# Down projection of an fp4-gated attention kernel: three of five full chunks per token tile as three one-pass products

## The chip, the cores and the metric

The kernel runs on one NeuronCore of a Trainium2 chip. The core has a matrix engine (PE, with its weight loads shown apart as PEld), a vector engine (DVE), a scalar engine (ACT), a general engine (POOL) and a queue engine (SP) that here issues nearly all DMA transfers. Each engine runs its own list of instructions in the order of the program and waits on semaphores for the others. The metric is the device time of one execution in microseconds (us). The kernel before was measured three times: 646.16, 646.59 and 648.52 us, median 646.59 us. A difference of some 0.5% (about 3 us) is what such a measurement can tell from none.

## What is computed

The input `x` has 4 batches of 2048 tokens with 256 values each. Layer normalisation gives `xn`. A linear attention with norms over the tokens gives `s`. A gated feed-forward net, all of whose operands are rounded block by block (16 values) to fp4, gives `g`; the result is `x + s * silu(g)`.

```python
def fp4_linear(x, w):
    xq = fp4_quant_dequant(x)
    wq = fp4_quant_dequant(w)
    return jnp.einsum('bsk,nk->bsn', xq, wq)
gate = fp4_linear(x, w_gate)
y = fp4_linear(x, w_up)
h = jax.nn.silu(gate) * y          # 704 values of a token
return fp4_linear(h, w_down)       # 704 -> 256
...
xn = _layernorm(x, axis=-1)
s = _L0_attn_ref(xn, ...)
g = _silu(_L0_ffn_ref(xn, ...))
x = x + s * g
```

A rounded value is a block's scale (its largest magnitude over 6) times one of fifteen grid values. The last line of the feed-forward net, the product with `w_down`, is the down projection that the change is about.

## The kernel before

**Tiling.** Tokens go in 32 groups of 256 (`N` = 32), each as two token tiles of 128 (`T` = 2); eight groups make a batch. One step `s` of the main loop (line 1084) works on several groups at once: gate and up products of group `s+1`, scaling and rounding of `h` of group `s-1`, the down projection of group `s-3`, layer normalisation and the Gram matrix of group `s+3`, the attention's product for group `s-7`. Loops are written out in full, and each engine's order is the order of the text, by hand.

**Gate and up.** A group has six pieces (3 chunks of weights by 2 token tiles), u0 to u5. From group 6 on all of them run as products of exact parts: `x = a + b` with `a` its upper part (a product with `1 - 2**-13`, stored in the one-pass format fp32r), `m = a - 4096 b`, and likewise for the weights. `gu_begin` (line 532) issues four one-pass products (a with the first part, b with the second, for two halves of the 256 values), then ACT scales the PSUM bank in place by `1 + 1/4096` (line 550); `gu_end` (line 553) adds two products with `m` and ACT takes silu (line 570). Then `h` is the product of the two halves, on DVE (`times_up`, line 581) for the first pieces and on POOL (line 577) for the last two.

**h.** `scale_h` (line 445) takes the largest magnitude of each block (line 165, DVE), the inverse scales (lines 174 and 178), and writes the scaled `h` into a tile `y` of its own (line 188), and with it the scaled `xn` of a later group. ACT shortens the upper halves of these words to 16 bits (`short_part`, line 227, three instructions), DVE rounds them to the grid (line 237). The scales themselves are transposed (`turn_scales`, line 464), written to DRAM, and read back by two broadcasts into the tile `se` (`spread_scales`, line 475): first the part for `xn` (256 KB), then that for `h` (704 KB). A step later `rescale_h` (line 521) transposes the eleven chunks of 128 values (two token tiles of five full chunks each, and one chunk shared by both) and multiplies them by `se` into `hqt` (line 527). `rescale_x` (line 496) does the same for `xn`, and `part_a`, `part_b`, `part_m` (lines 505 to 519) split it into the parts that the gate and up products take.

**Down projection.** `down` (line 609) takes for each token tile five plain fp32 products of 128 by 128 by 256, each of which the profile records as two instructions (line 617), and two one-pass products for the shared middle chunk (line 627), whose halves `part_middle` (line 593) has made with ACT and POOL. In the steady loop the parts of `down` stand at three places of the step: after the Gram matrix, before u2, and after u1's end. `gate_of` (line 636) takes silu out of PSUM. Five groups later `close` multiplies by the attention's result (line 676, DVE), POOL adds `x` (line 683), and SP stores.

**What sets the order around the change.** In one step DVE goes: the last part of `part_m`, the two reductions of `scale_h`, line 174, line 178, line 188 twice, `times_up` of u0, `close`, `times_up` of u1, `rescale_x`, `on_grid`, `times_up` of u2 and u3, `rescale_h`, `part_b`, `part_m`. ACT goes: the bank scaling of u0, `part_middle`, the bank scaling of u1, two sums of a later group, silu of u0, the transposed scales, `short_part` three times, the bank scaling of u2, silu of u1, and so on. Three steps out of eight carry a batch's attention algebra as well (`attention`, line 703, advanced by calls of `turn()`): its products, and on DVE its elementwise work, stand between `part_m` of one step and `scale_h` of the next.

**Buffers.** A tile name with `bufs` buffers is handed out again when all readers of the older tile are through; who writes the new tile waits for them. Before, `se`, `f`, and each of `xq0`, `xq1`, `xq2` (the parts a, b, m of `xn`) have two buffers, `hqt` one, `h` three.

## Time and profile before

| | |
|---|---|
| times | 646.16, 646.59, 648.52 us; median 646.59 us |
| span of the profiled execution | 647.0 us |
| busy: PE, DVE, ACT, POOL | 613.8, 477.7, 420.4, 183.7 us |
| mean granted clock of PE | 0.995 |
| a step without attention work | 17.0 us (start of line 638 at 343.99, 361.02, 378.08, 395.10 us) |
| the three steps with it | 21.23, 20.74, 20.97 us (line 638 at 412.23, 433.46, 454.20, 475.17 us) |
| products of line 617 / line 627 | 640 records / 128 records |

The page gives no time of its own for the profiled execution apart from the span, which lies 0.4 us above the median of the times. Times in the trace are from the start of the span. A record's duration reaches from its start to its modelled end; records of PE overlap, so the distance between starts, not the duration, says what a product costs in a stream.

### The profile page before, as it was taken

How to read it: one execution, taken by the hardware profiler on the slowest of the kernel's cores; microseconds unless marked ns; L12 is line 12 of the kernel's file. 1: busy time of each engine (PE TensorE's matmuls, PEld its weight loads, DVE VectorE, ACT ScalarE, POOL GpSimd, SP SyncE). 2: the span in 40 equal slices, each digit the busy share in tenths (PEclk: the TensorE clock that was granted, in tenths of full speed). 3: DMA queues.
4: the chain of work that ended last, by engine and by line, in shares of the span. 5: the costliest groups of instructions: out<-in, count | busy, mean ns of one | idle time of the engine just before them, and what ended most of it. 6: DMA issues, size and time to landing. Idle time of an engine off the chain costs nothing. (4 is left out here: it accounts for less than half of the span.)

```text
span 647.0 us, 9702 instructions
## 1 busy us (share of the span) xinstructions
PE 613.8 (95%) x3267; PEld 501.7 (78%) x3269; DVE 477.7 (74%) x942; ACT 420.4 (65%) x1108; POOL 183.7 (28%) x291
## 2 busy tenths in 40 slices
PE   4799898999899999999999999999999999999997
PEld 2446566778788888878788888878788888888886
DVE  6767767596777778596787868597786868686663
ACT  3457778666677777667677777756677766655431
POOL 4566684212122212112122222113122122113113
PEclk9899899999999999999999999999999999999999
DMA  9210043332233444442344444423443333322233
GB/s 208 89 34 16 19 102 94 79 81 60 57 88 111 115 111 112 115 90 70 73 112 113 114 115 113 109 60 75 101 115 98 97 94 103 92 67 67 83 94 131
DMA packets 29287, 59.47 MB, mean 92 GB/s; under 512 B 3541, under 2 KB 9909, under 8 KB 29237
## 3 DMA queue, kind: packets, MB, share of 16 engines
q1 hardware_dynamic: 28964, 58.59, 35.5%
q8 instruction: 26, 0.43, 0.3%
q10 hardware_dynamic: 272, 0.26, 0.1%
q14 instruction: 25, 0.20, 0.1%
HBM read 48.57 MB, written 10.27 MB: 91 GB/s over the span
## 5 line engine op out<-in xcount | busy, mean ns | idle before, releaser
L550 ACT ACTIVATE gu<-gu 128x512 f32<-128x512 f32 (+1 forms) x160 | 89.0, 556 | 139.8 <-PE gu L546 139.3
L546 PE MATMUL gu<-wgu,xq 128*128 128x512 f32 (+1 forms) x640 | 176.1, 397 | 2.8 <-DVE h L581 2.1
L617 PE MATMUL dn<-wdt,hqt 128*128 128x256 f32 x640 | 154.8, 382 | 0.5 <-ACT gate L1258 0.5
L577 POOL TENSOR_TENSOR h<-si,up 128x192 f32<-128x192 f32 (+1 forms) x92 | 67.0, 731 | 269.2 <-ACT up L576 269.1
L546 PEld LDWEIGHTS gu<-wgu,xq 128*128 128x128 f32 x640 | 113.2, 188 | 19.7 <-DVE h L581 3.2
L617 PEld LDWEIGHTS dn<-wdt,hqt 128*128 128x128 f32 x640 | 115.4, 190 | 16.5 <-ACT gate L1258 0.7
L581 DVE TENSOR_TENSOR h<-si,gu 128x256 f32<-128x256 f32 x100 | 41.8, 418 | 87.9 <-ACT si L570 87.9
L560 PE MATMUL gu<-wgu,xq 128*128 128x512 f32 (+1 forms) x320 | 99.5, 392 | 0.5 <-ACT gu L550 0.5
L570 ACT ACTIVATE si<-gu 128x256 f32<-128x256 f32 (+1 forms) x192 | 69.6, 363 | 19.6 <-PE gu L546 17.2
L683 POOL TENSOR_TENSOR gate<-gate,xl 128x512 f32<-128x512 f32 x27 | 34.5, 1278 | 120.6 <-issue 96.9
L560 PEld LDWEIGHTS gu<-wgu,xq 128*128 128x128 f32 x320 | 59.3, 188 | 10.5 <-ACT gu L550 1.6
L227 ACT ACTIVATE t_h<-y_h 128x704 f16<-128x704 bf16 (+2 forms) x86 | 60.7, 770 | 7.8 <-DVE y_h L188 7.7
L666 PE MATMUL at<-M,xnt 128*128 128x256 f32 x256 | 65.3, 384 | 0.0
L527 DVE TENSOR_TENSOR hqt<-tp_qh,se 128x1024 f32<-128x1024 f16 x64 | 53.8, 883 | 14.7 <-PE tp_qh L493 11.5
L398 PEld LDWEIGHTS gram<-xn 128*128 128x128 f32 x256 | 44.2, 194 | 15.9 <-ACT xn L373 8.2
L398 PE MATMUL gram<-xn 128*128 128x257 f32 (+1 forms) x256 | 48.7, 334 | 7.5 <-ACT xn L373 7.5
L546 PE MATMUL gu<-wp,xqt 128*128 128x512 f32 (+1 forms) x120 | 52.2, 581 | 2.2 <-ACT xqt L385 2.2
L188 DVE SCALAR_TENSOR_TENSOR y_h<-h,inv_h 128x1408 f32<-128x1408 f32 x32 | 53.5, 1671 | 1.1
L165 DVE TENSOR_REDUCE scs<-h 128x88 f32<-128x1408 f32 x32 | 51.5, 1610 | 0.0
L666 PEld LDWEIGHTS at<-M,xnt 128*128 128x128 f32 x256 | 45.9, 190 | 4.0
L601 POOL TENSOR_TENSOR both<-hqt,both 64x128 fp32r<-64x128 f32 x56 | 31.8, 568 | 42.8 <-ACT both L599 40.6
L546 PEld LDWEIGHTS gu<-wp,xqt 128*128 128x128 f32 x120 | 22.7, 199 | 23.1 <-issue 16.1
(176 smaller groups left out, 916.5 us busy)
## 6 DMA issues: line engine op xcount, KB each, us to landing
se<-there SPq DMA_DIRECT2D x32, 704.0 KB
x<-in_L_attn_x_dram SPq DMA_DIRECT2D x32, 256.0 KB
out_dram<-gate SPq DMA_DIRECT2D x31, 256.0 KB
se<-there SPq DMA_DIRECT2D x27, 256.0 KB
xl<-in_L_attn_x_dram SPq DMA_DIRECT2D x27, 256.0 KB
there<-sct SPq DMA_DIRECT2D x27, 60.0 KB
wd_n<-in_L_ffn_w_down_dram SPq DMA_DIRECT2D x1, 704.0 KB
wgu_n<-in_L_ffn_w_up_dram SPq DMA_DIRECT2D x2, 256.0 KB
```

What stands on the lines that cost most here:

```text
L165: nc.vector.tensor_reduce(sc, src.rearrange("p a (n k) -> p a n k", k=BLK), AX.X, ALU.max, apply_absolute_value=True)
L188: nc.vector.scalar_tensor_tensor(y.rearrange("p (a n k) -> p a n k", a=a, k=BLK), src.rearrange("p a (n k) -> p a n k", k=BLK), DOWN, inv. ...
L227: nc.scalar.activation(t[:, lo:hi], upper[:, lo:hi], AF.Copy, scale=ONE * (1.0 + 2.0**-8))
L398: nc.tensor.matmul(grams[b][:, o : o + L + 1 - c * P], xn[:, t, c * P : (c + 1) * P], xn[:, t, c * P : L + 1], start=(g == 0 and t == 0 an ...
L527: nc.vector.tensor_tensor(ht[:, cols], turn_chunks(q, g0, g1, f"h{n}"), spread_sc[n][:, cols], ALU.mult)
L546: nc.tensor.matmul(gu[:, : nb * P], x_k, w_k, start=(k == 0), stop=(k == len(pairs) - 1), skip_group_check=True)
L550: nc.scalar.activation(gu[:, : nb * P], gu[:, : nb * P], AF.Copy, scale=1.0 + 1.0 / STEP)
L560: nc.tensor.matmul(gu[:, : nb * P], xqt[n][2][:, t, c, :], wgu[2][:, c, cols], start=False, stop=(c == KC - 1), skip_group_check=True,)
L570: nc.scalar.activation(si[:, :nb, :], pair[:, :, 0, :], AF.Silu)
L577: nc.gpsimd.tensor_tensor(h, si[:, :nb, :], up[:, :nb, :], ALU.mult)
L617: nc.tensor.matmul(ods[n][:, t, :], hqt[n][:, t * (half + 1) + i, :], wdt[:, t * half + i, :], start=(i == 0), stop=False, skip_group_chec ...
L666: nc.tensor.matmul(ready[n][:, t, :], xnt[n][:, c, t * P : (t + 1) * P], M[:, c, :], start=False, stop=(c == KC - 1), skip_group_check=True,)
```

## The change

Of the five full chunks of each token tile three (`KX` = 3, so six of ten per group) are no longer plain fp32 products. Their `h` is split into exact parts as the gate and up products do it: `split_a` (ACT, 128x768), `split_b` (POOL, `h - a`) and `split_m` (DVE, `a - 4096 b`), and the weights into three parts (`split_d`, once, in the opening stage). The down projection of a group becomes `down_first` (six one-pass products per token tile), `down_scale` (ACT scales the PSUM bank in place by `1 + 1/4096`), and `down_rest` (two one-pass products for the middle chunk, two plain fp32 ones, three one-pass ones with `m`, per token tile). The first piece u1 is issued ahead of the first part of the down projection. Scaled `h` is written in place over `h`, so the tile `y` goes; scaled `xn` goes to a smaller tile. Buffers become single for `se`, `xq1`, `xq2`, and `f`, and the reading back of the scales moves behind `rescale_h`, the last reader of the older `se`. `rescale_h` writes two tiles with three instructions, chunks to be split first. At the end the two token tiles of the last group get a PSUM bank each.

```diff
@@ scale_h, spread_scales
-        y = tok.tile([P, NS * P], F32, tag="y", name=f"y_h{n}", bufs=1)[:, 0 : ng * P]
-        over(y[:, 0:HF], src, inv[:, 0 : NIC * CB])
+        y = src.rearrange("p t f -> p (t f)")
+        over(y, src, inv[:, 0 : NIC * CB])
...
-        se = tok.tile([P, most], F32, tag=tag, name=f"se_{key}", bufs=2 if tag == "se" else 3)[:, 0 : n * BLK]
+        se = tok.tile([P, most], F32, tag=tag, name=f"se_{key}", bufs=1 if tag == "se" else 3)
...
     def part(n: int, i: int):
-        return tok.tile([P, T * L], F32R, tag=f"xq{i}", name=f"xq{i}_{n}", bufs=2)
+        return tok.tile([P, T * L], F32R, tag=f"xq{i}", name=f"xq{i}_{n}", bufs=1 if i else 2)
...
+    def split_a(n: int, room=None):
+        hparts[n] = part_room(n, room)
+        nc.scalar.activation(hparts[n][0], hqt[n][0], AF.Copy, scale=SHORT)
+
+    def split_b(n: int, engine):
+        a, b = hparts[n][0:2]
+        engine.tensor_tensor(b, hqt[n][0], a.bitcast(F32), ALU.subtract)
+
+    def split_m(n: int):
+        a, b = hparts[n][0:2]
...
+        nc.vector.scalar_tensor_tensor(m, b.bitcast(F32), -STEP, a.bitcast(F32), ALU.mult, ALU.add)
...
+    def down_first(n: int, t: int, tile=None):
...
+        for i in range(KX):
             for k in range(2):
+                kk = t * KX + i
                 nc.tensor.matmul(
+                    od,
+                    hparts[n][k][:, kk * P : (kk + 1) * P],
+                    wdk[k][:, kk, :],
...
+    def down_scale(n: int, tile=None):
+        od = ods[n] if tile is None else tile
+        nc.scalar.activation(od, od, AF.Copy, scale=1.0 + 1.0 / STEP)
+
+    def down_rest(n: int, t: int, tile=None):
+        od = ods[n][:, t, :] if tile is None else tile
+        pairs = [(over_lower[n][:, t, :], wde[:, k, t, :]) for k in range(2)]
+        for i in range(KX, HALF):
...
+        for i in range(KX):
+            kk = t * KX + i
+            pairs.append((hparts[n][2][:, kk * P : (kk + 1) * P], wdk[2][:, kk, :]))
...
+    def split_d(engine):
+        for place, w in whole_d.items():
...
+            nc.scalar.activation(c, w, AF.Copy, scale=SHORT)
+            engine.tensor_tensor(w, w, c.bitcast(F32), ALU.subtract)
+            nc.scalar.activation(d, w, AF.Copy, scale=STEP)
+            engine.tensor_tensor(w, d.bitcast(F32), c.bitcast(F32), ALU.subtract)
+            nc.scalar.activation(m, w, AF.Copy, scale=1.0 / STEP)
+            yield
@@ the opening stage
+    lower = split_d(nc.gpsimd)
...
     next(parts)
+    next(lower, None)
     gate_up(3, 0, 1)
     gate_up(3, 1, 1)
+    next(lower, None)
...
     gate_up(3, 1, 2)
+    for _ in lower:
+        pass
     gram_step(5)
     turn_xn(5)
...
@@ the loop over s
+        u1 = gu_begin(*pairs[1])
         if s > 3:
-            down(s - 3, 0)
-        u1 = gu_begin(*pairs[1])
+            down_first(s - 3, 0)
...
             turn_scales(s - 1)
-            spread_scales(s - 1)
-            shorts()
+            short_h(s - 1, y_h, th)
...
-            down(s - 3, 1)
+            down_first(s - 3, 1)
+            down_scale(s - 3)
+            split_m(s - 3)
...
-        down(s - 3, 0 if s == 3 else 2)
-        down(s - 3, 1 if s == 3 else 3)
+            down_rest(s - 3, 0)
+            down_rest(s - 3, 1)
...
         rescale_h(s - 2)
+        spread_scales(s - 1)
         if parts_x:
             part_b(s + 2, xs)
             part_m(s + 2, xs)
...
         h4 = gu_end(u4, s > 3 and 4 in direct)
+        split_a(s - 2)
+        split_b(s - 2, nc.gpsimd)
```

## The prediction

> **What bounds the kernel now.** I read the page first: PE is busy 95% of the span, no other engine over 74%, and PE's row of the slices stands at 9 nearly throughout. The chain of waits that ended last names only the last 30 us, so the steady loop is read from the timeline of one step. The lines below, from the page and from that timeline (start, time, engine, line; a row may merge several records), carry it.

> ```profile
> PE 613.8 (95%) x3267; PEld 501.7 (78%) x3269; DVE 477.7 (74%) x942; ACT 420.4 (65%) x1108; POOL 183.7 (28%) x291
> ```

> ```profile
> 382.22 0.70 PE L560 MATMUL gu<-wgu,xq 128*128 128x384 f32 x2
> ...
> 382.83 0.97 DVE L518 SCALAR_TENSOR_TENSOR xq<-xq,xq 128x512 fp32r<-128x512 f32 x1
> ...
> 383.72 1.61 DVE L165 TENSOR_REDUCE scs<-h 128x88 f32<-128x1408 f32 x1
> ...
> 387.15 1.62 DVE L188 SCALAR_TENSOR_TENSOR y_h<-h,inv_h 128x1408 f32<-128x1408 f32 x1
> ...
> 387.86 0.58 ACT L550 ACTIVATE gu<-gu 128x512 f32<-128x512 f32 x1 [1.38 <-PE gu L546]
> ...
> 389.71 1.99 ACT L227 ACTIVATE t_h<-y_h 128x704 f16<-128x704 bf16 x3
> ...
> 390.96 2.38 PE L617 MATMUL dn<-wdt,hqt 128*128 128x256 f32 x10
> ...
> 391.59 0.59 ACT L550 ACTIVATE gu<-gu 128x512 f32<-128x512 f32 x1
> ...
> 392.99 0.58 PE L627 MATMUL dn<-wde,both 128*128 128x256 f32 x2
> ...
> 393.41 1.09 PE L546 MATMUL gu<-wgu,xq 128*128 128x512 f32 x4
> ...
> 399.23 0.70 PE L560 MATMUL gu<-wgu,xq 128*128 128x384 f32 x2
> ```

> PE has no bracket anywhere: nothing holds it, and a step (17.03 us) is its work. DVE and ACT do have idle time (14.6 and 12.7 us busy of 17.0 by the windows). But DVE runs from line 518 straight through the reductions to line 188 with no gap, and ACT's line 227 starts only after that. Today PE's second half of the down projection (390.96) starts before line 227 is done (391.70): it needs nothing from it.

> **Products.** Records of line 617 follow each other at 0.216 us, two a chunk: 0.432. The pair of line 627 takes 393.41 - 392.99 = 0.42, of which the last record of line 617 still uses 0.19: some 0.117 each. Three one-pass products are 0.351, so a chunk gains 0.081, six chunks 0.49 us a group. If PE alone decided, steps would be 16.54.

> **The new wait.** `down_rest` adds into the bank that `down_scale` has scaled, and on ACT `down_scale` stands behind the three instructions of line 227, which wait for line 188, which stands on DVE behind `part_m` of the step before. `part_m` now writes a single-buffered `xq2`, so it waits for u5's last product. This closes a loop, by the rows above:
> - u5's products end at 382.92, handover 0.04;
> - DVE from the start of line 518 to the end of the large line 188: 387.15 - 382.83 + 1.62 = 5.94;
> - handover 0.04, then ACT from 389.71 to the next instruction at 391.59: 1.88;
> - `down_scale`, priced as line 550, 0.59, handover 0.04. So far 8.53;
> - `down_rest`: ten one-pass products (1.17) and four fp32 chunks (1.73): 2.90;
> - PE from 393.41 to u5's end at 399.93: 6.52.

> The sum is 17.95 us a step. PE's own way from u5's end to this place is 390.96 - 382.92 = 8.04, less 2.38 (five fp32 chunks, two one-pass products) plus 1.40 (twelve one-pass products) = 7.06; so PE waits 1.5 us there, and about 0.5 of that is its own saving. A second loop is as long: `times_up` of u3 starts at 397.20 and `part_m` at 399.85; `rescale_h` takes 0.95 + 0.55 + 0.41 in place of 1.22 + 0.55, +0.14, which puts `part_m` at 9.48 after the start of `down_rest`, against 9.46 by the first. Undoing the single buffer alone would therefore not help. I take 18.0, +1.0 a step. It is bounded below by +0.6 (handovers overlap, DVE's starts overlap by 0.08 more) and above by +1.6 (next paragraph).

> **The other added work of a step.** `split_a`: line 507 (512 wide) 0.64 and the slope of line 227 (1.39 at 1408, 0.79 at 704) give 0.86 on ACT. It lands where ACT idles before u1 (the bracket of 1.38, which moving u1 ahead removes too). If that cover is gone, line 227 starts late by the difference. Counting ACT's work from silu of u4 to line 227 plus both new instructions ends within 0.1 of DVE's chain, so ACT is a third candidate, already at the limit. `split_m`: lines 518 and 188 (0.69 at 512, 1.62 at 1408) give 0.96, behind line 188, in DVE's idle time (1.84 in the step shown); if not hidden, `times_up` of u3 comes later by what sticks out. `split_b`: POOL's rows (0.59 at 192, 1.27 at 512) give 1.82. Behind `part_m` it runs from 1.0 to 2.9 us after u5's end; `down_first` comes at 3.4 (the Gram products end at 385.44, 2.5 after 382.92, and u1 takes 0.93). Behind it on POOL are u5's `h`, read a step later, and `part_middle`, wanted by `down_rest` at 8.5. POOL and DVE get in each other's way: line 518 takes 0.69 where POOL is idle (458.12) and 0.97 beside line 577, and a line 347 of 0.16 took 1.12 beside POOL's 1.27 of line 683. From none to 0.6 a step, hence the upper bound; I take what is in the rows of line 518 already.

> [...]

> **SP.** The two broadcasts move past `store`'s wait and now wait for `rescale_h`; behind them stand the output store, the next two loads and the scales' write. The loads are read a step later. The last group's 704 KB went out at 625.90 and its reader started at 634.29: 8.4 us. The 256 KB part is wanted some 9.5 us after issue, the rest after 15. I cost this at nothing; late data would hold `rescale_x`, microsecond by microsecond.

> **Attention steps.** DVE's algebra lies inside the loop. Line 518 at 416.99 and the reduction at 422.90 are 5.91 apart, at 458.12 and 464.49 6.37, against 0.89. That makes 17.95 + 5.02 = 22.97 against 21.23, and 23.43 against 20.97. In the step between, no algebra precedes the reduction; PE is busy 20.1 of 20.7, so I take +0.6. Sum +4.8, taken as 5 a batch; the first batch (longer PE steps, fp32 pieces) 3, the last (two steps and the end) 4: +17, bounds 8 and 22.

> **The opening.** From the timeline:

> ```profile
> 76.21 1.79 POOL L917 TENSOR_TENSOR wde<-all_ends,wde 128x512 fp32r<-128x512 f32 x1 [3.63 <-ACT wde L916]
> ...
> 77.69 0.62 ACT L885 ACTIVATE wgu<-rest_G 128x512 fp32r<-128x512 f32 x1
> ...
> 79.08 0.39 ACT L570 ACTIVATE si<-gu 128x256 f32<-128x256 f32 x1 [0.77 <-PE gu L546]
> ...
> 85.13 0.59 ACT L382 COPY xnt<-tp_xn 128x512 f32<-128x512 f32 x1
> ...
> 85.77 0.77 PE L493 MATMUL tp_qh<-ident,t_h 128*128 128x128 bf16 x11 [0.56 <-ACT xnt L382]
> ```

> The reader is to see that PE there waits for ACT's line 382. `split_d` puts three blocks ahead of it, each ACT, POOL, ACT, POOL, ACT with ACT blocked in between: 3 x 0.64 + 2 x 1.27 + handovers = 4.6 us, 13.8 in all. ACT idles some 1.9 us there now, so line 382 comes 12 us later; PE's products of that stretch end at 86.7 at the latest and wait. I take +11.5, bounds 5 (half is caught up by engines that ran ahead) and 15 (POOL's line 882 took 1.7 to 2.7 beside DVE).

> **The end.** The last group adds `split_a` 0.86, `split_b` and `split_m` (DVE) and a scaling, but its second tile no longer waits for the first one's gate (0.5 at 640.27) and 2.4 us of products become 1.45: by the same sums -0.5, within 2 either way.

> **Sum.** 15 plain steps +15, attention +17, opening +11.5, end -0.5: +43. The span was 647.0, 0.4 above the median of the runs: 690.

> **Rivals.**
> - *PE decides after all*: `down_scale` is through before PE asks, and the opening costs its lower bound. 28 groups x -0.49 = -14, +5: 638. For it: PE is the only full engine. Against: the loop of 8.53 must shrink by 1.5 us, and each piece is a measured duration in a fixed order. It decides only if line 227 starts before 388.2 on the clock above.
> - *Hidden*: steps gain 0.3 over before, opening 5, attention 3: 660. For it: ACT and DVE have idle time. Against: their order.
> - *POOL's `split_b` falls on `part_m` or line 188*: another 1.2 a step over 27 steps: 722. For it: the 1.12 of line 347. Against: POOL's `h` of u4 goes first and `part_m` is through before.
> - *One-pass products no faster in a stream* (0.19, a weight load's duration): 6 x 0.14 more behind the wait, 27 x 0.4, 701. The 0.117 of line 627 speaks against it; it lies in the range.

> **Numbers.** Forecast and the last rival 0.76, PE decides 0.08, hidden 0.04, POOL 0.10, no difference that a measurement here can tell (0.5%) 0.02. The range adds the bounds: 690 - 6 - 9 - 6.5 = 668, 690 + 9 + 5 + 3.5 = 708; I widen it to 662, into the hidden case. Faster 0.08, same 0.02, slower 0.90.

> **What would show it.** Right: plain steps of about 18.0; each with PE idle about 1.5 us ahead of the first product of `down_rest`, ended by ACT's scaling of `dn`; line 227 still starting at the end of line 188; one gap of about 12 us on PE near 87 us, ended by line 382. Wrong: no idle time ahead of `down_rest`; steps of 16.5; PE's gap ended by POOL or a DMA.

## The result, and the profile after

The changed kernel takes 720.04 us (median of 4 executions, 718.91 to 723.55) against 647.22 us (4 executions, 646.16 to 648.52) for the kernel before on the same chip: a ratio of 1.113, 95% interval 1.110 to 1.117. The forecast was 690 us, 662 to 708: the right sign, the mechanism of the steady step as described, and 30 us too little. Left out of the times and ratios below are three executions at a clearly lower granted clock than their kernel's others: two of run 11 (755.5 and 755.9 us, 0.939 against 0.949) and one of run 12 (791.3 us, 0.755 against 0.993 to 0.997).

Line numbers below are those of the changed kernel. The ones that matter: 623 the first four products of a gate and up piece, 627 ACT's scaling of its bank, 171, 180, 184, 194 the reductions, inverse scales and large scalings of `scale_h`, 247 ACT's shortening, 402 and 405 ACT's copies of transposed tiles, 543 `part_m`, 573 and 583 `rescale_h`, 596, 600, 607 `split_a`, `split_b`, `split_m`, 654 POOL's product for `h`, 676 and 678 `part_middle`, 696 `down_first`, 707 `down_scale`, 719 `down_rest`, 723 the gate's silu.

The page, first its busy times, then a row of the forty slices (the clock granted to PE, in tenths):

```profile
PE 619.5 (86%) x3461; PEld 508.1 (71%) x3461; DVE 519.5 (72%) x1008; ACT 465.2 (65%) x1187; POOL 277.9 (39%) x328
...
PEclk9999979999999999999999999999999999999999
```

PE fell from 95% of the span to 86%. It is busy 619.5 us, not less than before (613.8), though every group's products became shorter. The row of the clock points to the reason: the sixth slice has a 7, and single windows of half clock elsewhere, 3.41 us each, are too short to change a digit. The mean granted clock went from 0.995 to 0.972. Of PE's busy time 33.8 us lie in half-clock windows, against 6.0 before; half of the difference, 13.9 us, an estimate of what it cost (four records below take 1.86 us there and 1.03 at full clock), is more than the 5.7 us by which the busy time rose.

The timeline of one plain step (start, time, engine, line; a bracket is idle time before it and what ended it):

```profile
433.40 0.90 DVE L543 SCALAR_TENSOR_TENSOR xq<-xq,xq 128x512 fp32r<-128x512 f32 x1
...
436.46 0.40 DVE L180 TENSOR_SCALAR scs<-scs 128x120 f32<-128x120 f32 x1
...
437.83 1.62 DVE L194 SCALAR_TENSOR_TENSOR h<-h,inv_h 128x1408 f32<-128x1408 f32 x1
...
439.22 0.26 ACT L405 ACTIVATE sct<-tp_sc 120x128 f32<-120x128 f32 x1
...
439.49 1.47 ACT L247 ACTIVATE t_h<-h 128x704 f16<-128x704 bf16 x2
...
441.39 0.58 ACT L707 ACTIVATE dn<-dn 128x512 f32<-128x512 f32 x1
...
442.11 0.47 PE L719 MATMUL dn<-wde,both 128*128 128x256 f32 x2 [1.50 <-ACT dn L707]
...
445.09 1.10 PE L623 MATMUL gu<-wgu,xq 128*128 128x512 f32 x4
...
451.67 0.90 DVE L543 SCALAR_TENSOR_TENSOR xq<-xq,xq 128x512 fp32r<-128x512 f32 x1
```

This is the loop of the forecast, piece by piece: `part_m` to line 194 takes 4.43 us, to line 247 1.66, to `down_scale` 1.90, to the first product of `down_rest` 0.72, that stretch 2.98, and on to the next `part_m` 6.58: 18.27 us, where the forecast had 17.95. PE waits 1.50 us, ended by ACT's line 707.

ACT's own queue is as long as DVE's chain here, as the forecast had feared: line 405 ends at 439.48, line 194 on DVE at 439.45. Which of the two sets the step, this step alone can't say. A later one does: there ACT waits 0.74 us for line 194, and from `part_m` to `part_m` (575.95 to 594.22) it still takes 18.27 us. So DVE's chain is enough to set it.

```profile
582.04 1.47 ACT L247 ACTIVATE t_h<-h 128x704 f16<-128x704 bf16 x2 [0.74 <-DVE h L194]
```

In the list of waits (total, times, longest) PE's wait for line 707 is its largest by far, once in each step of the loop:

```profile
PE dn L719 <- ACT dn L707: 45.5, 28, 3.2
```

The opening:

```profile
79.99 0.63 ACT L1020 ACTIVATE wdk<-wd 128x512 fp32r<-128x512 f32 x1 [1.38 <-POOL wd L1019]
...
96.88 0.57 ACT L402 COPY xnt<-tp_xn 128x512 f32<-128x512 f32 x1
...
97.50 1.33 PE L517 MATMUL tp_qh<-ident,t_h 128*128 128x128 bf16 x11 [10.88 <-ACT xnt L402]
...
113.12 0.47 PE L719 MATMUL dn<-wde,both 128*128 128x256 f32 x2 [3.20 <-ACT dn L707]
```

The transposes of `h` start at 97.50 in place of 85.77, 11.7 us late behind ACT's line 402, as forecast (11.5). But there is a second wait of 3.20 us in the loop's first step, which the forecast did not have.

Where the 72.3 us of span came in is read from the starts of the gate's silu (line 638 before, 723 after), group by group: how much later each is than its counterpart.

| stretch | forecast | measured |
|---|---|---|
| opening and the loop's first step (group 0's gate +16.7, group 1's +3.7) | +11.5 | +20.4 |
| first three attention steps | +3 | +9.6 |
| second three | +5 | +8.6 |
| third three | +5 | +6.0 |
| last attention work | +4 | +3.0 |
| 15 plain steps | +15 | +20.4 |
| end | -0.5 | +4.2 |
| sum | +43 | +72.3 |

The second and third batch do the same work, and differ by 2.6 us. First a place just ahead of each batch, where PE waited 1.86 us both times:

```profile
295.83 0.47 PE L719 MATMUL dn<-wde,both 128*128 128x256 f32 x2 [1.86 <-ACT dn L707]
296.14 1.86 PE L719 MATMUL dn<-wdt,hr 128*128 128x256 f32 x4
...
460.84 0.48 PE L719 MATMUL dn<-wde,both 128*128 128x256 f32 x2 [1.86 <-ACT dn L707]
461.16 1.03 PE L719 MATMUL dn<-wdt,hr 128*128 128x256 f32 x4
```

The same four records take 1.86 us in the one and 1.03 in the other. Stretches of equal length, each from some 3.8 us ahead of the row with the wait (length, then busy time of PE, PEld, DVE, ACT and POOL, the granted clock, and the transfers):

```profile
292.00:326.10 34.10, 28.60 (x149) 23.96 (x149) 24.18 (x65) 19.66 (x52) 8.22 (x8) 0.91 0.34 84
457.00:491.10 34.10, 28.59 (x165) 24.00 (x164) 25.77 (x69) 21.10 (x56) 8.25 (x8) 1.00 0.34 84
```

PE is as busy in both, with 16 records fewer done in the first: its clock was 0.91 there.

Four questions remained for the runs: is the wait for `down_scale` really what sets the step (theory A) or does something else follow close behind; where do the opening's other 9 us come from; what do the attention steps pay for; and what is the half clock worth (theory C).

### The profile page after: what moved, and what is told of

Its sections match the earlier page's. It is cut to its first block, busy times and chain, and to the rows that moved or that the text cites. A ratio compares the mean times of both kernels' runs of the same rounds, so it can differ in the third digit from the quotient of the medians.

```text
span 719.3 us, 10378 instructions
## 1 busy us (share of the span) xinstructions
PE 619.5 (86%) x3461; PEld 508.1 (71%) x3461; DVE 519.5 (72%) x1008; ACT 465.2 (65%) x1187; POOL 277.9 (39%) x328
## 4 chain that ended last, share of the span: by engine, by line
PE 50%; DVE 21%; ACT 20%; issue 4%; POOL 4%; DMA 1%; SPq 0%; ACTq 0%; POOLq 0%; DVEq 0%
PE gu L623 15%; PE dn L719 13%; PE gu L637 6%; PE at L750 5%; DVE scs L171 5%; DVE h L194 4%; ACT t_h L247 3%; PE tp_qh L517 3%; ACT xn L393 2%; ACT xn L337 2%; DVE inv_h L184 2%; PE dn L696 2%; ACT dn L707 2%; ACT hp L596 2%; ACT gu L627 2%
## 5 line engine op out<-in xcount | busy, mean ns | idle before, releaser
L627 ACT ACTIVATE gu<-gu 128x512 f32<-128x512 f32 (+1 forms) x160 | 87.7, 548 | 147.9 <-PE gu L623 147.8
L719 PE MATMUL dn<-wde,both 128*128 128x256 f32 x124 | 28.5, 313 | 46.2 <-ACT dn L707 45.5
L678 POOL TENSOR_TENSOR both<-hr,both 64x128 fp32r<-64x128 f32 x56 | 52.2, 932 | 40.1 <-ACT both L676 37.6
L600 POOL TENSOR_TENSOR hp<-hk,hp 128x768 fp32r<-128x768 f32 x29 | 64.5, 2223 | 6.1 <-ACT hp L596 5.3
L719 PE MATMUL dn<-wdt,hr 128*128 128x256 f32 x240 | 65.4, 397 | 0.0
L623 PE MATMUL gu<-wp,xqt 128*128 128x512 f32 (+1 forms) x120 | 54.1, 596 | 3.6 <-ACT xqt L405 2.2
L247 ACT ACTIVATE t_h<-h 128x704 f16<-128x704 bf16 x64 | 47.1, 784 | 15.3 <-DVE h L194 15.1
L719 PEld LDWEIGHTS dn<-wde,both 128*128 128x128 f32 x124 | 20.0, 199 | 51.6 <-issue 46.4
L194 DVE SCALAR_TENSOR_TENSOR h<-h,inv_h 128x1408 f32<-128x1408 f32 x32 | 53.1, 1658 | 1.1
L696 PE MATMUL dn<-wdk,hp 128*128 128x256 f32 x348 | 53.5, 290 | 0.2 <-POOL hp L600 0.2
```

What stands on the lines that cost most here:

```text
L194: nc.vector.scalar_tensor_tensor(y.rearrange("p (a n k) -> p a n k", a=a, k=BLK), src.rearrange("p a (n k) -> p a n k", k=BLK), DOWN, inv. ...
L247: nc.scalar.activation(t[:, lo:hi], upper[:, lo:hi], AF.Copy, scale=ONE * (1.0 + 2.0**-8))
L623: nc.tensor.matmul(gu[:, : nb * P], x_k, w_k, start=(k == 0), stop=(k == len(pairs) - 1), skip_group_check=True)
L627: nc.scalar.activation(gu[:, : nb * P], gu[:, : nb * P], AF.Copy, scale=1.0 + 1.0 / STEP)
L696: nc.tensor.matmul(od, hparts[n][k][:, kk * P : (kk + 1) * P], wdk[k][:, kk, :], start=(i == 0 and k == 0 and (t == 0 or tile is not None) ...
L719: nc.tensor.matmul(od, h_k, w_k, start=False, stop=(k == len(pairs) - 1), skip_group_check=True)
```

## Experiments

All times are medians of 4 executions (2 in the eleventh run, 9 in the twelfth). Runs 1 to 4, 5 to 8 and 9 to 12 ran on three different chips, each time beside the kernel before (646.92 to 647.27 us); across them the ratios are the better measure. Runs 1 to 5 and 11 start from the changed kernel, run 12 from the kernel before. "Later" by a group's gate means later than in the trace of the kernel before.

**1. `down_first` and `down_scale` ahead of the shortening.** Only the order of the text changes: ACT scales the bank before line 247.

```diff
         if s > 3:
+            down_first(s - 3, 1)
+            down_scale(s - 3)
             turn_scales(s - 1)
             short_h(s - 1, y_h, th)
...
         if s > 3:
-            down_first(s - 3, 1)
-            down_scale(s - 3)
             split_m(s - 3)
```

> The changed kernel with the second part of down_first and down_scale issued ahead of the transposed scales and the three shortening instructions, so that on ACT down_scale no longer stands behind them; everything else as changed. Theory A (the step is set by the loop DVE reductions - line 194 - shortening - down_scale - down_rest): the loop is cut, plain steps fall from 18.27 us to PE's own work, 17.03 - 0.49 = 16.5 to 16.7 us, PE's idle time of 1.5 us ahead of down_rest goes, and with it 27 x 1.6 = 43 us or more: some 672 to 678 us, with the opening's loss kept. Rival B (DVE and POOL, in each other's way since split_b came, set the step): steps stay within 0.3 us of 18.27, about 715 us.

Measured: 690.12 us, ratio 1.066 (1.063 to 1.070). Plain steps fall from 18.27 to 16.68 and 17.16 us by turns (before: 17.04), so the loop is cut and theory A stands for them. But the total missed 672 to 678: the first attention step of each batch takes 27.0 to 27.1 us (24.6 to 26.7 in the changed kernel, 20.9 to 21.2 before). The timeline there:

```profile
306.54 0.95 DVE L607 SCALAR_TENSOR_TENSOR hm<-hp,hp 128x768 fp32r<-128x768 f32 x1
...
307.54 1.01 PE L719 MATMUL dn<-wdk,hm 128*128 128x256 f32 x3 [2.91 <-DVE hm L607]
...
308.78 1.91 PE L719 MATMUL dn<-wdt,hr 128*128 128x256 f32 x4
```

`down_rest` now waits in its middle, for `split_m`, which stands on DVE behind the attention's algebra and the scaling of `h`; and half clock follows (four records in 1.91 us; the clock is 0.50 from 306.78 to 313.60 us). One wait was taken away and the next one, hidden until then, came out.

**2. `split_d` in three stages.** ACT does the first parts of all three blocks, then the second, then the third, as `split_gu` does, instead of waiting for POOL twice in each block.

```diff
         for place, w in whole_d.items():
...
+            c, d, m = of(place)
             nc.scalar.activation(c, w, AF.Copy, scale=SHORT)
             engine.tensor_tensor(w, w, c.bitcast(F32), ALU.subtract)
+        yield
+        for place, w in whole_d.items():
+            c, d, m = of(place)
             nc.scalar.activation(d, w, AF.Copy, scale=STEP)
...
```

> The changed kernel with the weights' split in three stages (three upper parts; three scaled remainders; three last parts) at the same three places of the opening, so that ACT does not wait for POOL inside a stage; the loop as changed. Theory A (ACT, held by POOL, delays line 402 and with it PE; a part of the rest is the clock that falls while PE waits): PE's idle 10.88 us near 87 us shrinks to under 4, no half clock for 10 us there; the first gate comes 8 to 12 us earlier than at 116.6; total 720 - 10 = 708 to 712. Rival B (the opening is late for other reasons, the added work itself): less than 4 us gained.

Measured: 713.85 us, ratio 1.103 (1.100 to 1.105), 6.2 us less and short of the 708 to 712 expected. Group 0's gate comes 8.4 us later than before instead of 16.7. Of these 8.3 us some 2.2 are not the edit's: the traces before and after have a half-clock window near 20 us (from 19.88 and 19.71 us), this one has none, and line 991, ahead of `split_d`, already starts at 63.19 us instead of 65.35. So the wait of ACT for POOL was worth some 6 us.

**3. Both edits.** The diffs of runs 1 and 2 together.

> The changed kernel with both edits: down_scale ahead of the shortening, and the weights' split staged. Theory A: the two add up, 720 - 45 - 10 = 665 or less; steps of 16.5 to 16.7 us would give 647 - 13 = 634 plus what the opening and the attention steps still cost (5 to 20): 635 to 655. Rival B: 700 or more.

Measured: 680.22 us, ratio 1.054 (1.048 to 1.059). The two add up (690.1 - 6.2 = 683.9 expected from the single runs), but the range of 635 to 655 was far off: the waits for `split_m` (14.2 us in all), a first gate still 10.4 us late and an end some 5 us longer come to more than the 5 to 20 us it allowed.

**4. Zeros in the opening's wait.** 46 products of zeros keep PE busy while it waits for ACT, so that its clock is full when the transposes of `h` start. Nothing else changes.

```diff
     turn_scales(1)
+    keep_busy(46)
     rescale_h(0)
```

> The changed kernel with 46 products of zeros on PE (512 wide, 0.216 us each, 9.9 us) where PE otherwise idles for 10.88 us in the opening; no other change. Theory A (part of the opening's loss is the granted clock, at half from 91.4 to 101.6 us because PE idled): the clock stays at 1.0, the products after 97.5 us run at full speed, and the first gate comes 1.5 to 2.5 us earlier: 718. Rival B (the clock has no part in it): the same time within 0.5 us, or later if the zeros are in the way.

Measured: 721.69 us, ratio 1.115 (1.113 to 1.118): no gain, against the expectation. The half clock of 10.2 us from 91 us on is gone, yet `down_rest` starts at the same time:

```profile
89.78 7.07 PE L740 MATMUL zero_at<-zero 128*128 128x512 bf16 x32
97.85 0.77 PE L517 MATMUL tp_qh<-ident,t_h 128*128 128x128 bf16 x11 [1.00 <-ACT xnt L402]
...
113.19 0.77 PE L719 MATMUL dn<-wde,both 128*128 128x256 f32 x2 [4.90 <-ACT dn L707]
113.75 1.91 PE L719 MATMUL dn<-wdt,hr 128*128 128x256 f32 x4
```

113.19 against 113.12: PE merely waits 4.90 us instead of 3.20, and now this longer wait is followed by half clock, and the first gate comes 2.7 us later than in the changed kernel. So PE's speed does not set the start of `down_rest` there; that it is `down_scale` behind line 247, as in the other steps, is tested by run 7.

**5. Zeros in the waits of the loop.** Six products of zeros, added into the open Gram bank, ahead of each `down_rest`, and five ahead of the attention's `pm`.

```diff
+    def fill(b: int, count: int):
+        for _ in range(count):
+            nc.tensor.matmul(
+                grams[b][:, 0:512], zero[:, 0:P], zero, start=False, stop=False, skip_group_check=True
+            )
...
+            fill(b + 1, 5)
...
+            if s + 3 < N:
+                fill((s + 3) // NG, 6)
             down_rest(s - 3, 0)
```

> The changed kernel, with six products of zeros added into the open Gram bank ahead of each down_rest, and five ahead of the products pm of the attention (they add zero). Theory C, the clock has a price of its own: in the profile of the changed kernel half-clock windows of 3.41 us come after waits of PE of 1.9 us and more, at 132, 160, 194, 296, 324 and 358 us. The second batch of attention steps, with three of them, came out 8.6 us longer than before, the third, with none, 6.0: 0.85 us a window. With zeros in the waits these windows go, plain steps stay at 18.27, and the time falls by some 5 us, to 715 (713 to 717). Rival: PE waits anyway, and half clock only uses up waiting time: 720, within 1. A third: the zeros run on past the wait and PE comes late: over 721, with steps over 18.3.

Measured: 715.64 us, ratio 1.105 (1.101 to 1.109), 4.4 us less than the changed kernel for 165 products more. Every half-clock window between 118 and 690 us is gone (mean granted clock 0.981 in place of 0.972). The attention steps of the second and third batch now both cost 6.05 us, where they cost 8.6 and 6.0; those of the first 7.6 instead of 9.6; one plain step that had cost 3.2 us more than before costs 1.6, and the step from group 0's gate to group 1's 1.5 us less. Plain steps without a window stay at 18.3, so the zeros cost nothing and the loop is untouched. That is theory C: the waits of PE that half clock followed were paid a second time. It had reckoned with 0.85 us a window, from three windows in the second batch; two lie there, and they cost 2.5 us.

**6. `split_m` ahead of the reductions.** From here on each run adds to run 3. In the first attention step of each batch `split_m` goes between the attention's algebra and `scale_h`.

```diff
+        if s % NG == 5:
+            split_m(s - 3)
...
         y_h = scale_h(s - 1, s + 3)
...
-        if s > 3:
+        if s > 3 and s % NG != 5:
             split_m(s - 3)
```

> The kernel with both edits (down_scale ahead of line 247, split_d in stages: 680.2), and split_m ahead of the reductions in the second step of each batch, the one in which PE waited 2.9 to 3.9 us for the products of hm. Theory A: split_m stands behind the attention's algebra on DVE; ahead of it by 4.5 us of reductions and scaling, that wait goes, this step falls from 24.6 to 22 or less, and with it the half-clock windows that follow: 680 - 3 x 2.6 = 672 (669 to 675). Rival B: DVE's own chain decides that step, 0.96 us more lies ahead of the reductions, and what the products gain line 247 and the next step lose: 678 to 681.

Measured: 672.27 us, ratio 1.038 (1.036 to 1.041): theory A, within a microsecond. The step falls from 24.6 to 22.8 us (in the first batch from 27.1 to 23.7), the half-clock windows between 111 and 649 us go (mean granted clock 0.985, 0.972 in run 3), and PE's waits for `hm` shrink from 14.2 us in all (longest 3.9) in run 3 to this:

```profile
PE dn L719 <- DVE hm L607: 3.0, 8, 0.5
```

**7. The same order in the loop's first step.** `down_firsts(0)` moves ahead of `short_h(2)`.

```diff
         if s == 3:
             h1 = gu_end(u1)
+            down_firsts(0)
             short_h(2, y_h, th)
```

> As the run before, and in the first step of the loop down_first and down_scale of group 0 ahead of line 247 as well, where PE waited 3.4 us for down_scale at 100.7 us. Theory A: the first gate comes 3.4 us earlier and the time falls by as much, 668.5 if the run before gives 672. Rival B: ACT and DVE are late there on their own account (DVE's large scaling took 2.37 us beside POOL in place of 1.62, the next 1.75 in place of 0.69), the next step takes back what this one gains: within 1 us of the run before.

Measured: 664.53 us, ratio 1.027 (1.023 to 1.032): 7.7 us less, twice what theory A gave. The 3.5 us wait of PE is down to 0.3, and a half-clock stretch of 6.8 us behind that wait is gone with it (mean granted clock 0.987 in place of 0.985). The first gate comes 5.2 instead of 10.7 us late; as this trace has the window near 20 us and that of run 6 does not (line 991 starts at 65.49 and 63.91), the edit is worth some 7 us there. Its four executions spread from 662.9 to 668.8 us.

**8. `split_b` at the end on DVE, ahead of `part_middle`.** In group 30 it moves from POOL to DVE; in group 31 it was on DVE, and only the order changes.

```diff
-    split_b(n - 1, nc.gpsimd)
+    split_b(n - 1, nc.vector)
     part_middle(n - 1, nc.vector)
...
+    split_b(n, nc.vector)
     part_middle(n, nc.vector)
-    split_b(n, nc.vector)
```

> As the run before, and in the end split_b of group 30 on DVE in place of POOL, ahead of part_middle, and split_b of the last group ahead of part_middle. PE waited there 1.65 us for split_a and 1.5 us for split_b, and a half-clock stretch of 6.8 us followed. Theory A: split_b takes about 0.9 on DVE in place of 1.8 on POOL, part_middle loses the 2.1 us it took beside POOL, and the half clock goes: 1.5 to 4 us less than the run before. Rival B: the end is set by the chain through the last group's scales and broadcast, and nothing changes: within 0.7.

Measured: 664.20 us, ratio 1.025 (1.022 to 1.028): no difference from run 7 that the times can tell, as rival B had it. The traces do show an end 2.0 us shorter (counted from group 28's gate): PE's wait for `split_b` is 0.6 us in place of 1.5, the half-clock window near 645 us is gone (mean granted clock 0.989 in place of 0.987), and the wait of 1.65 us for `split_a` stays.

**9. `split_m` directly behind `scale_h` in all other steps.** In run 8 every second plain step still takes 17.16 us; small DVE instructions of the layer normalisation stand ahead of `split_m` there, and PE waits for it (0.30 us at 369.10).

```diff
         y_h = scale_h(s - 1, s + 3)
+        if s > 3 and s % NG != 5:
+            split_m(s - 3)
         little(3)
```

> As the run with the edits in the opening, the first step and the end (664.2), and split_m directly behind the scaling of h in every step, ahead of the small deviation instructions and of line 658. In that run plain steps alternate between 16.68 and 17.16; in the longer ones PE waits 0.3 us for the products of hm, behind small DVE instructions. Theory A: the long steps fall to 16.7 as well, 12 x 0.48 less: 658.5 (657 to 661). Rival B: line 658 of u0 now comes 0.95 us later on DVE, and the products of u3 wait for its bank instead: 664, within 1.

Measured: 660.57 us, ratio 1.020 (1.016 to 1.023), 3.6 us less by the medians; the intervals of runs 8 and 9 just touch, so the size is uncertain. In the traces the gain is plain: 12 of the 15 plain steps now take 16.57 to 16.65 us, and the one ahead of each batch's attention 17.16, 17.00 and 16.69. That is theory A in kind, short of its 5.7 us. Part of the rest may be the clock: the profile of run 8 has one half-clock window between 100 and 650 us, that of run 9 has four (mean granted clock 0.989 and 0.982). The windows of a plain step in the kernel before and in this one:

```profile
372.00:389.00 17.00, 17.00 (x99) 14.63 (x97) 11.95 (x18) 12.64 (x36) 3.63 (x5) 1.00 0.46 109
```

```profile
372.00:388.60 16.60, 16.60 (x104) 14.59 (x103) 14.41 (x25) 13.82 (x38) 7.30 (x6) 1.00 0.46 112
```

PE is busy all of the time in both: with the order mended PE decides again, and a plain step gains 0.45 us where the forecast's products gave 0.49.

**10. Without `split_m`.** The third product of a chunk takes the first part of `h`; `m` is not computed.

```diff
     def split_m(n: int):
...
+        hparts[n] = [hparts[n][0], hparts[n][1], hparts[n][0]]
```

> As the run before, but split_m is left out and the third product of a chunk takes the first part of h in place of the mixed one, so this part of the computation is not done. It shows what the rest of the change costs when its last instruction on DVE is free. Theory A: with the order mended only steps of attention and the end still pay for split_m: plain steps stay at 16.7, the time is 3 to 6 us below the run before, still above 647. Rival B: DVE's load is what keeps the steps of attention above those before: 10 us or more below, at or under 647.

Measured: 658.19 us, ratio 1.017 (1.012 to 1.021). That is 2.4 us less than run 9, a little under theory A's 3 to 6, and the two intervals overlap: once it stands in a good place, `split_m` costs little, if anything that can be told. Rival B, 10 us or more, falls.

**11. `split_b` of the loop on DVE.** From the changed kernel, one word changed: 0.95 us more on DVE inside the loop, and POOL free of 2.2 us a step.

```diff
         split_a(s - 2)
-        split_b(s - 2, nc.gpsimd)
+        split_b(s - 2, nc.vector)
```

> The changed kernel with one edit: split_b of the loop on DVE, where it stands behind part_m and ahead of the reductions, in place of POOL. By the loop of the prediction (what lies on DVE between part_m and the large scaling is on the path) a plain step of 18.27 grows by the 0.9 that 768 elements take on DVE, less what POOL's work now costs DVE: 19.2 if that is nothing, and 720 + 27 x 0.9 = 744 us. If POOL's split_b costs DVE as much as the prediction's upper bound, 0.6 a step, 18.6 and 729. If the loop is not what decides, 18.3 and 720.

Measured: 744.34 us (743.9 and 744.8), ratio 1.150 (1.146 to 1.154): the 744 expected for a loop in which POOL's work costs DVE nothing. The trace is of an execution of 755.5 us; what it shows of DVE's chain says that this agreement is partly luck:

```profile
256.23 0.90 DVE L543 SCALAR_TENSOR_TENSOR xq<-xq,xq 128x512 fp32r<-128x512 f32 x1
257.05 0.95 DVE L600 TENSOR_TENSOR hp<-hk,hp 128x768 fp32r<-128x768 f32 x1
...
260.16 0.22 DVE L180 TENSOR_SCALAR scs<-scs 128x120 f32<-128x120 f32 x1
...
261.35 1.62 DVE L194 SCALAR_TENSOR_TENSOR h<-h,inv_h 128x1408 f32<-128x1408 f32 x1
```

From `part_m` to line 194 it is 5.12 us instead of 4.43: `split_b` adds 0.87 between starts and line 180 gives 0.18 back (0.22 instead of 0.40). The 0.40 is not beside `split_b` itself (433.72 to 435.99) but beside POOL's line 654, which comes after it on POOL, waited another 0.20 us for ACT's line 653, and ended at 436.79, 0.07 us ahead of line 180's own end. Throughout the changed kernel's trace line 180 takes 0.38 to 0.42 us beside line 654 in the plain steps, but for the last two, where line 654 is nearly through when it starts: there it takes 0.22, and a step takes 18.09 us instead of 18.27. So the 0.18 us go with line 654, whose start ACT sets there, and not with `split_b`; in this run line 180 starts 3.93 us after `part_m` instead of 3.06. The loop grows by 0.69: 27 x 0.69 would be 739 us. Where the other 5 us come from is not shown. The granted clock of the two executions of 744 us, 0.949 against 0.972, would fit more half clock, but no trace of them exists.

**12. The single buffer alone, in the kernel before.**

```diff
-        return tok.tile([P, T * L], F32R, tag=f"xq{i}", name=f"xq{i}_{n}", bufs=2)
+        return tok.tile([P, T * L], F32R, tag=f"xq{i}", name=f"xq{i}_{n}", bufs=1 if i else 2)
```

> The kernel before with one edit: one buffer in place of two for the second and third part of x, as the changed kernel has it, so that part_b and part_m wait for the products of the step before. By the prediction the single buffer closes the loop only together with the wait of down_rest for down_scale; here nothing on PE waits for line 227 in the same step, and the time stays at 647, within 2. Rival: the single buffer by itself delays the scaling of h and with it the next step: 1 us a step, 665 to 675.

Measured: 647.27 us, ratio 1.000 (0.998 to 1.002). Waiting for u5 by itself cost nothing here (647.27 us before as well); that it would matter where PE in turn waits, in the same step, for what DVE does after it, is the forecast's estimate. Two buffers in the changed kernel were not tried, so the forecast's second loop, of the same length without the single buffer, was not tested.

## Why the prediction was right or wrong

The sum missed 29.3 us (72.3 of span against 43): 11.2 in the three batches' attention steps, 8.9 in the opening and the loop's first step, 5.4 in the plain steps, 4.7 at the end, less 1.0 in the last attention work. The step that failed is how the steady step's wait was carried to the other places: `split_m` behind the attention's algebra, `down_scale` in the loop's first step and the splits of groups 29 and 30 at the end had no price of their own, and no wait was charged for the half clock that followed it.

**Products: right.** -0.49 us a group forecast, -0.45 measured in run 9, where nothing else holds PE. The rival of one-pass products no faster falls.

**The new wait: right in place and cause, 0.24 us a step too small.** PE idles 1.50 us ahead of `down_rest`, ended by ACT's scaling of `dn`, and run 1 ended it by order alone. As the order of run 1 frees the scaling from DVE's chain and from ACT's queue alike, it is the later step with ACT waiting that names DVE. Against the 17.95 us of the sum, the loop takes 18.27; 0.11 more lies on DVE, where line 180 took 0.40 us (0.22 in run 11), 0.09 on the handover of `down_scale`, 0.08 in `down_rest`, and 0.04 elsewhere. `split_b` itself took 2.27 us, not 1.82. Its price to the step was bounded by 0 and 0.6 and taken as what the rows of line 518 had in them. The plain steps show none beyond that: what DVE lost there beside POOL, the 0.18 us of line 180, it lost beside line 654, which waited 0.20 us for ACT after `split_b` had ended. (The row of line 518 at 458.12, read as one with POOL idle, has POOL's line 577 beside it from 458.52 on.) DVE also lost outside the loop, a small instruction taking 1.14 us beside POOL's addition:

```profile
442.74 1.28 POOL L767 TENSOR_TENSOR gate<-gate,xl 128x512 f32<-128x512 f32 x1 [2.96 <-issue]
...
442.91 1.14 DVE L367 SCALAR_TENSOR_TENSOR isq_yp<-isq_rp,isq_yp 128x4 f32<-128x4 f32 x1
```

The rest of the plain steps' +20.4 is 1.6 us in one step with a half-clock window. The rival that put `split_b` on `part_m` at 1.2 us a step (722 us) came near the measured time for a wrong reason: `part_m` took 0.90 us beside `split_b` (433.40) and 0.90 in run 11, where `split_b` comes after it on DVE.

**Attention steps: the term was mis-sized, and part of it had no term.** 3, 5 and 5 us were forecast. With full clock (run 5) they cost 7.6, 6.05 and 6.05. In the changed kernel half clock adds 2.0 and 2.5 us to the first two batches and nothing to the third. The third batch shows the terms apart: its last attention step takes 23.40 us, where the forecast had 23.43, the middle one 0.2 more than before in place of 0.6, and the first one 24.64 in place of 22.97. There DVE's algebra keeps `part_m` and the reduction 6.49 us apart (470.42 to 476.91), not 5.91; the loop's base is 18.27, not 17.95; and PE waits a second time, for `split_m`, which was taken to fit into DVE's idle time:

```profile
486.56 0.62 PE L719 MATMUL dn<-wdk,hm 128*128 128x256 f32 x3 [0.60 <-DVE hm L607]
```

With the scaling moved ahead (runs 1 and 3) this wait grew to 2.9 us and more, and run 6 took it away by order alone. The first batch was wrong by more: its "longer PE steps" were taken to hide the wait for `down_scale`, and in its first step in run 5 PE still waited 1.16 us for it and 0.60 for `split_m`. That step cost 4.6 us more than before, the batch's last one 2.4, as in the third batch.

**The opening: the term was right, its place in a sum was not.** ACT's line 402 came 11.7 us late (11.5 forecast). The failing step is that after this lag the loop's first step was costed at nothing. There `down_scale` stands behind line 247 as in every other step, and PE waited 3.2 us more. And DVE reaches the end of line 194 later: from the first row of `rescale_h` 11.84 us in place of 9.07, as `split_m`, with a wait for POOL's `split_b`, stands ahead of the reductions:

```profile
102.36 0.96 DVE L607 SCALAR_TENSOR_TENSOR hm<-hp,hp 128x768 fp32r<-128x768 f32 x1 [1.71 <-POOL hp L600]
```

Run 2 takes 6.2 us off the time, run 7 another 7.7 by the medians; run 4 shows that PE's clock did not set the start of `down_rest` at this place.

**The end: right for the last group, and two groups had no term of their own.** -0.5 forecast, +4.2 measured from group 28's gate. The last group, the only one that the forecast summed, gained 1.0 us. Groups 29 and 30 lost 2.2 and 3.0: PE waits 1.51 us at 681.09 for line 180 of the last group's scales, and in group 30 for `split_a` and `split_b`, and a half-clock window follows.

```profile
696.80 0.38 PE L696 MATMUL dn<-wdk,wgu 128*128 128x256 f32 x1 [1.65 <-ACT wgu L596]
...
698.68 2.51 PE L696 MATMUL dn<-wdk,wgu 128*128 128x256 f32 x11 [1.50 <-POOL wgu L600]
```

Moving `split_b` to DVE (run 8) shortened the end in the trace by 2.0 us, but not the times by anything that can be told, so what decides the end stays open.

**SP: costed at nothing, and nothing was seen.** In the loop of the changed kernel no wait of an engine ends on a DMA; the two in the trace that do, 3.60 and 1.53 us, end at 3.60 and 6.71 us.

**What had no step at all: PE's clock.** The kernel before has 2 windows of half clock, both ahead of the loop; the changed one has 12, counting the opening's stretch as three, and six of them stand in the loop, each behind a wait of PE of 1.86 us or more (2.97, 2.45, 2.35, 1.86, 2.13 and 1.98). The forecast counted waits of PE as time lost once. By the gates, from group 0's on, the zeros of run 5 took 7.5 us off the loop for these six, some 1.2 us each (the median fell by 4.4, as the opening of that trace was longer).

**What would have made it faster than before?** With the order of runs 1, 2, 6, 7, 8 and 9 the ratio falls from 1.113 to 1.020, but not below 1. By the same gates run 9 has 14.9 us of span more than before: 4.8 in the opening, 5.0, 3.6 and 3.8 in the three batches, 3.7 with the last attention work and the end, less some 6 for the plain steps. The products' whole saving, 28 groups x 0.45 = 12.6 us, is smaller than the 20.9 us that the other places lost. How much of these is the splitting itself is not shown; `split_m` alone is at most a few us of them (run 10).

## To carry over

Before an in-place scaling (or any new dependency between two engines) is put into a hand-ordered loop, follow what its engine has queued ahead of it and what those wait for: here three instructions behind the slowest DVE chain turned a 17.0 us step into an 18.3 us cycle, and moving the scaling ahead of them gave the plain steps that back. When one wait is removed, look at once for the next one at the same consumer, and cost a stall of PE twice: its length, and some 1.2 us more for the half clock that followed here behind six of eleven waits of 1.86 us or more. A saving of products is worth what the steps bound by PE take of it, so the extra work's way through opening, odd steps and end has to be summed as carefully as the steady step.

## What the hardware showed

**DVE instructions took longer beside POOL's.** A DVE instruction on 4 values a partition (line 367, at 442.91) took 1.14 us beside POOL's 1.28, and 0.16 in the median of 24. Line 180 took 0.40 beside line 654 and ended 0.07 after it; in run 11 it took 0.22. At 680.03 it took 0.91 beside `split_b`, again ending 0.07 after it, and 0.21 at 688.85 with POOL idle. In the plain steps of the loop, but for the last two, line 180 lost 0.18 us a step.
